# Modulated norms that take 1 + scale ahead of the inverse root, modulation weights in two loads, ones added on ScalarE, and a new hand-set priority table: an adaLN transformer block on one core

## The chip, the cores and the metric

The kernel runs on one core of a Trainium2 chip. Time is device time in microseconds (us) of that core. A profiled execution gives, beside the time, a trace with every instruction of TensorE (PE, with its weight loads as PEld), VectorE (DVE), ScalarE (ACT), GpSimd (POOL) and SyncE (SP, which only issues transfers here). All arithmetic that matters here is float32. One matmul of the program shows as two records in the trace: 87 fillers of the program are 174 records.

## The reference

Eight sequences of 1024 tokens by 128 features go through an attention stack of six layers and a quantized feed-forward part. Each part has a modulated norm in front and a gate behind; scale, shift and gate come from a conditioning vector of the sequence:

```python
mod = (_silu(L0_c) @ L0_wmod).reshape(L0_c.shape[0], 6, 1, -1)
sa, ca, ga, sb, cb, gb = (mod[:, 0], mod[:, 1], mod[:, 2], mod[:, 3], mod[:, 4], mod[:, 5])
...
h = _layernorm(x, axis=-1) * (1 + ca) + sa
x = x + ga * _L0_attn_ref(h, ...)
h = _layernorm(x, axis=-1) * (1 + cb) + sb
x = x + gb * _L0_ffn_ref(h, ...)
```

The attention part is six layers of norm, linear attention, norm and a two-layer MLP; the feed-forward part rounds blockwise to FP4 ahead of each of three matmuls. The modulated norm is thus computed twice for each sequence: once at its start, once ahead of the quantized part. The twelve norms inside the attention stack are plain ones whose weight and bias are folded in later.

## The kernel before

**Tiling.** One sequence is "a batch b" here. Its 1024 tokens are eight chunks of 128 tokens, and a half (h = 0, 1) is four chunks, so a half is a tile of 128 partitions by 512. Four batches are in flight at a time in four sets of buffers ("lanes"); the fifth to eighth reuse them.

**Order of the work.** The kernel does not issue its instructions as it describes them. Every step is put into a `Plan` with its engine, an estimated duration and what it reads and writes (`add`, L96). `Plan.order` (L143) then runs a list scheduler over these estimates. Of the steps that could start first it takes the one with the longest remaining chain plus a hand-set bonus. The bonuses are `LEAD[b][stage]`, changed at set times by `TURNS` (L291 to L360); a batch has eight stages: 0 is its modulated norm, 1 to 6 are the layers, 7 is the quantized part. The order that comes out is fixed: every engine runs its own list strictly in that order, and waits for what the others owe it.

**Fillers.** Where the scheduler expects PE to sit idle longer than `GAP` (0.6 us, half of that up to time `COLD`), it puts in matmuls of the identity by itself, whose result nobody reads (`warm`, L1348). They keep PE running while it has nothing to do. Fillers too are fixed parts of the list: PE runs them even if real work is ready earlier.

**The parts that the change touches.**
- The loads (L448 to L451): the conditioning vector, the first half of batch 0, all of the modulation weights `wmod` (384 KB), the second half of batch 0. All go out from the one SP queue, in this order, then every other weight.
- `prepare_mod` (L517): the modulation of all eight sequences as rows of 8 partitions. Two DVE instructions (L538) add 1 to the scales.
- `first_modulation` (L856): for the first four batches, scale and shift spread over the partitions by a matmul of `wmod`'s first 256 columns (L862), with two copies on ACT (L870, L871) that also add the 1.
- `layernorm` (L614): statistics on DVE (L630, L636), the inverse root as a logarithm and an exponential on ACT (L650, L655) and a correction of three small DVE instructions (L660, L665, L670), a fourth for the shift (L676); then the norm is applied, in chunks of 128 columns, by DVE (L682, mean and inverse root as two per-partition scalars) or by ACT (L689). The plain norms share a half between the two.
- `modulated_norm` (L887): a `layernorm`, then a multiply by 1 + scale on DVE over the whole half (L893) and an add of the shift on POOL (L901). At a batch's start the half is shared between DVE and ACT; ahead of the quantized part all four chunks are ACT's (the argument `HV` is 0).

```python
for h in range(H):
    layernorm(ln, dst, src, h, name, HV)
    add("DVE", vec(HW), ... tensor_tensor(half(dst, h), half(dst, h), over(mod[:, n + 1], HC), ALU.mult) ...)
    add("POOL", 1.2,    ... tensor_tensor(half(dst, h), half(dst, h), over(mod[:, n], HC), ALU.add) ...)
```

Of the kernel before, what the change touches and what calls it, by code (L numbers as in the profile page):

```python
# [11 lines left out]
ALU = mybir.AluOpType  # L12
# [71 lines left out]
class Plan:  # L84


    LAT = {"PE": 0.31, "ACT": 0.14, "DVE": 0.125, "POOL": 0.04, "SP": 2.0}
    SEE = {"PE": 0.015, "ACT": 0.0, "DVE": 0.0, "POOL": 0.1, "SP": 0.0}

    GAP, BRINK, COLD = 0.6, 0.15, 7.5  # L90

# [144 lines left out]
def mm(n):  # L236

    return 0.01 + n * 1.66e-3


def move(kb):

    return max(0.45, kb * 4.0e-3)

# [5 lines left out]
def kernel(  # L250
# [40 lines left out]
    LEAD = [  # L291
        [2420, 4178, 586, 336, -1174, -1157, -1341, -3664],
        [158, 557, 2162, 224, -3448, -84, 492, -1524],
        [1202, -253, -1456, -2344, -3625, 1683, -2362, -2313],
        [-238, 636, -1421, 177, -416, 253, -5410, -152],
# [7 lines left out]
        (15, [(2, 1, -124)]),  # L303
        (45, [(0, 2, 1600), (3, 0, -324)]),
        (60, [(1, 1, -935)]),
        (75, [(0, 3, 1449), (1, 1, 557), (3, 1, 592)]),
        (90, [(3, 1, 2100)]),
        (120, [(3, 2, 2464), (3, 3, 2879)]),
        (135, [(0, 3, 3161)]),
        (150, [(1, 1, 2636)]),  # L310
        (165, [(1, 2, 3857)]),
        (195, [(0, 4, 1947)]),
        (210, [(1, 3, 1937)]),
        (225, [(0, 4, 2875), (0, 6, 2412), (0, 7, 99)]),
        (240, [(2, 1, -1301), (3, 3, 1394)]),
        (255, [(0, 5, 2591), (1, 3, 3015), (1, 4, -653)]),
        (270, [(3, 4, 2428)]),
        (345, [(0, 6, 2433), (4, 0, -1503)]),
        (390, [(1, 4, -2461)]),
        (405, [(3, 6, -3105)]),  # L320
        (435, [(1, 4, -3419)]),
        (450, [(3, 6, -3090)]),
        (465, [(2, 2, 551), (2, 4, -3123), (3, 6, -3105)]),
        (510, [(4, 1, -3111)]),
        (525, [(3, 6, -3271)]),
        (540, [(3, 6, -3110)]),
        (600, [(3, 7, 2098)]),
        (615, [(2, 4, -3534)]),
        (630, [(2, 6, -2208), (5, 1, 1840)]),
        (660, [(5, 1, 1745)]),  # L330
        (690, [(5, 1, 2562)]),
        (720, [(4, 3, -2144)]),
        (750, [(2, 6, -2203)]),
        (780, [(2, 6, -2201), (2, 7, -2144), (4, 3, -2142), (5, 4, -2397)]),
        (810, [(2, 7, -2186)]),
        (825, [(3, 7, -2164), (4, 3, -1269)]),
        (840, [(3, 7, -2468)]),
        (870, [(3, 7, -340)]),
        (885, [(3, 7, -553), (4, 4, 939), (4, 5, 1955)]),
        (915, [(5, 4, -1086), (6, 2, -534)]),  # L340
        (945, [(4, 6, 1221)]),
        (975, [(4, 7, -240), (7, 1, -1371)]),
        (990, [(6, 3, 282)]),
        (1005, [(4, 7, -743), (5, 4, -650)]),
        (1035, [(4, 7, -1539), (5, 5, -1458)]),
        (1050, [(5, 5, -591), (6, 3, 867), (6, 4, 1080), (7, 2, 307)]),
        (1095, [(6, 4, -754)]),
        (1110, [(6, 4, -1551)]),
        (1125, [(4, 7, -4373), (6, 4, -758)]),
        (1140, [(6, 5, -1624)]),  # L350
        (1200, [(5, 7, -1877)]),
        (1215, [(6, 5, -185), (7, 4, -2011)]),
        (1230, [(6, 5, -1795)]),
        (1245, [(6, 6, -373), (7, 5, -366)]),
        (1260, [(6, 6, -371), (7, 5, -372)]),
        (1275, [(6, 6, -365), (7, 5, -367)]),
        (1305, [(6, 7, -440), (7, 6, -443)]),
        (1320, [(7, 6, 40)]),
        (1335, [(4, 7, -2064), (5, 7, -2271), (6, 7, -2282), (7, 6, 278), (7, 7, 207)]),
    ]  # L360
# [88 lines left out]
    load_x(0, 0)  # L449
    load(lambda: wmod_b.ap()[:, :NM], wmod, [wmod_b], 384)  # L450
    load_x(0, 1)  # L451
    for n, src in enumerate((ln1_w, ln1_b, ln2_w, ln2_b)):
        load(lambda n=n: rows[n * L : (n + 1) * L, :], src, [("rows", n)], 3)
# [63 lines left out]
    def prepare_mod():  # L517
        for o, e in MS:
            u = Ps(psum)
            add(  # L520
                "PE", mm(e - o),
                lambda u=u, o=o, e=e: nc.tensor.matmul(
                    u.ap()[:B, : e - o], cT, wmod_b.ap()[:, o:e],
                    start=True, stop=True,
                ),
                r=["cT", wmod_b], w=[u],
            )
            add(
                "ACT", act(e - o),
                lambda u=u, o=o, e=e: nc.scalar.copy(flat8[:, o:e], u.ap()[:B, : e - o]),  # L530
                r=[u], w=[("mod8", o)],
            )

        shaped = [("mod8", o) for o, _ in MS]
        for n in (1, 4):
            add(
                "DVE", 0.14,
                lambda n=n: nc.vector.tensor_scalar(  # L538
                    mod8[:, n, :], mod8[:, n, :], 1.0, None, ALU.add
                ),  # L540
                r=shaped, w=[("mod", n)], port=True,
            )
# [70 lines left out]

    def layernorm(ln, dst, src, h, n, HV=HC // 2):  # L614

# [5 lines left out]

        def s(c):
            return chunks(half(src, h))[:, c, :]

        def d(c):
            return chunks(half(dst, h))[:, c, :]

        for c in range(HC):
            add(
                "DVE", 0.197, lambda c=c: nc.vector.bn_stats(stats.ap()[:, c, :], s(c)),  # L630
                r=at(src, h)[c * H // HC :][:1], w=[stats[c]],
            )

        def moments():
            for c in range(HC):
                nc.vector.bn_aggr(mv.ap()[:, c, :], stats.ap()[:, c, :])  # L636

        add("DVE", HC * 0.067, moments, r=[stats], w=[mv])

# [3 lines left out]
        def var():  # L643
# [27 lines left out]
            r=[shift], w=[rstd], port=True,  # L671
        )

        add(
            "DVE", 0.07,
            lambda: nc.vector.scalar_tensor_tensor(z(), mean(), -1.0, y(), ALU.mult, ALU.mult),  # L676
            r=[mv, rstd], w=[shift], port=True,
        )

# [7 lines left out]
        def apply_s():  # L687
# [8 lines left out]
            "ACT", (HC - HV) * (act(D, 2) + 0.04), apply_s, r=[*at(src, h), shift, rstd],  # L696
            w=[high] if HV else [low, high],
        )
        if HV:
            add("DVE", HV * 0.256, apply_v, r=[*at(src, h), mv, rstd], w=[low], port=True)  # L700

# [13 lines left out]
    def fp4(src, parts, ncol, n, i, last="POOL"):  # L715
# [13 lines left out]
        def each(t):  # L729
# [49 lines left out]
        add(  # L779
            last, (vec if last == "DVE" else pool2)(ncol),  # L780
            lambda: eng.tensor_tensor(blocks(src()), blocks(vv()), each(s()), ALU.mult),
# [74 lines left out]
    def first_modulation(mod, b):  # L856


        t = Ps(psum)
        add(  # L860
            "PE", mm(2 * D),
            lambda: nc.tensor.matmul(  # L862
                t.ap()[:, : 2 * D], cT[:, b : b + 1].to_broadcast([P, P]),
                wmod_b.ap()[:, : 2 * D], start=True, stop=True,
            ),
            r=["cT", wmod_b], w=[t],
        )

        def spread():
            nc.scalar.copy(mod.ap()[:, 0, :], t.ap()[:, :D])  # L870
            nc.scalar.activation(mod.ap()[:, 1, :], t.ap()[:, D : 2 * D], AF.Identity, bias=1.0)  # L871

        add("ACT", 2 * act(D), spread, r=[t], w=[mod[0]], func="exp")
# [12 lines left out]

    def modulated_norm(ln, dst, src, mod, n, name, HV):  # L887

        for h in range(H):
            layernorm(ln, dst, src, h, name, HV)  # L890
            add(
                "DVE", vec(HW),
                lambda h=h: nc.vector.tensor_tensor(  # L893
                    chunks(half(dst, h)), chunks(half(dst, h)),
                    over(mod.ap()[:, n + 1, :], HC), ALU.mult,
                ),
                r=[mod[n // 3]], w=at(dst, h), port=True,
            )
            add(
                "POOL", 1.2,  # L900
                lambda h=h: nc.gpsimd.tensor_tensor(  # L901
                    chunks(half(dst, h)), chunks(half(dst, h)),
                    over(mod.ap()[:, n, :], HC), ALU.add,
                ),
                r=[mod[n // 3]], w=at(dst, h),
            )

# [18 lines left out]
    def layer(x, b, l, ln, mod):  # L926
# [197 lines left out]
        if l == L - 1:  # L1124
# [3 lines left out]
            add(  # L1128
                "POOL", pool2(NJ * D) + 0.1,
                lambda: nc.gpsimd.tensor_tensor(  # L1130
# [4 lines left out]
            for h in range(H):  # L1135
# [8 lines left out]
                add(  # L1144
                    "POOL", pool2(HW) + 0.2,
                    lambda h=h: nc.gpsimd.tensor_tensor(
# [44 lines left out]
    def ffn(x, mod, b, ln):  # L1191
        hq = big(ln, "A", f"h_{b}")
        modulated_norm(ln, hq, x, mod, 3, f"f{b}", 0)
        hT = big(ln, "B", f"hTf_{b}")
# [123 lines left out]
    for b in range(B):  # L1318
# [11 lines left out]
        x = big(ln, "X", f"x_{b}")  # L1330
        modulated_norm(ln, x, x0s[b], mod, 0, f"i{b}", HC // 2)
        for l in range(L):
# [77 lines left out]
```

## Time and profile before

| what | value |
|---|---|
| median of 3 runs | 1406.71 us (1405.73 to 2585.54) |
| the profiled execution, time | 1406.12 us |
| its span, first to last instruction | 1404.4 us |
| PE busy | 1391.3 us, 99% |
| DVE, ACT, POOL busy | 1142.5 us (81%), 983.0 us (70%), 247.7 us (18%) |
| granted TensorE clock | 0.999 |
| fillers | 174 records (87 matmuls) |
| PE idle over the span | 1404.4 - 1391.3 = 13.1 us |

The span is the time between the first and the last instruction that the profile holds; the time of the run is 1.7 us longer. Busy shares are averages over stages with different limits: at the start DVE is the fuller engine, from about 47 us on PE hardly pauses. A PE that is busy can be busy with fillers, which are not work.

### The profile page before, as it was taken

The page shows a single profiled execution, that of the slowest core. Times are in us where ns is not written, and L with a number is a line of the kernel's source. Part 1 is how long each engine was busy: PE and PEld are TensorE (multiplying, and loading weights), DVE is VectorE, ACT ScalarE, POOL GpSimd, SP SyncE. Part 2 cuts the span into 40 slices and gives each one's busy share as a digit, 9 for nine tenths or more (in the row PEclk, how much of TensorE's full clock was granted, in tenths as well). Part 3 has the DMA queues.
Part 4 walks back from the last instruction along what each step waited for, and adds up shares of the span by engine and source line. Part 5 has one row for each costly group of instructions (what it writes and reads, how often), then busy time and mean ns, then how long its engine had stood idle before and what let it go on. Part 6 is the DMA issues. An engine that isn't in the chain of part 4 may idle for free.

```text
span 1404.4 us, 26348 instructions
## 1 busy us (share of the span) xinstructions
PE 1391.3 (99%) x9181; PEld 1116.3 (79%) x9181; DVE 1142.5 (81%) x4506; ACT 983.0 (70%) x2292; POOL 247.7 (18%) x216
## 2 busy tenths in 40 slices
PE   8999999999999999999999999999999999999998
PEld 6788779688768888688788778788787787887887
DVE  8998668487798687899667899988876748879897
ACT  6777666766686686767666668876776757777774
POOL 2211001001122020312101122211210101212232
PEclk9999999999999999999999999999999999999999
DMA  7100000000000000100000000000000000000001
GB/s 218 47 1 1 2 1 1 0 1 1 17 12 16 1 2 1 42 16 13 2 0 1 16 13 16 1 16 1 1 1 1 1 1 1 2 1 1 9 17 38
DMA packets 16293, 18.79 MB, mean 13 GB/s; under 512 B 1584, under 2 KB 10392, under 8 KB 16160
## 3 DMA queue, kind: packets, MB, share of 16 engines
q1 hardware_dynamic: 16160, 17.10, 3.9%
q8 instruction: 73, 1.20, 0.4%
q14 instruction: 60, 0.49, 0.1%
HBM read 12.88 MB, written 4.22 MB: 12 GB/s over the span
## 4 chain that ended last, share of the span: by engine, by line
PE 88%; DVE 7%; ACT 2%; SPq 1%; DMA 1%; issue 1%; POOL 0%; POOLq 0%; ACTq 0%; DVEq 0%
PE ps L1178 22%; PE ps L1161 22%; PE ps L708 11%; PE ps L1048 6%; PE ps L938 5%; PE ps L1115 5%; PE ps L985 5%; PE ps L1222 5%; PE ps L1302 3%; PE ps L1278 1%; SPq L417 1%; DVE x L1100 1%; PE ps L1082 1%; PE ps L1057 1%; DMA x<-in_L_attn_x_dram 1%; DVE stats_m L630 1%
## 5 line engine op out<-in xcount | busy, mean ns | idle before, releaser
L1161 PE MATMUL ps<-xT_m,w_sb 128*128 128x512 f32 x768 | 352.0, 595 | 0.3 <-ACT xT_m L918 0.3
L1161 PEld LDWEIGHTS ps<-xT_m,w_sb 128*128 128x128 f32 x768 | 137.6, 191 | 128.8 <-issue 95.6
L1026 POOL TENSOR_TENSOR q<-q,qsum 128x512 f32<-128x512 f32 x96 | 102.4, 1075 | 709.2 <-DVE qsum L1021 377.2
L1100 DVE TENSOR_TENSOR x<-ps,x 128x512 f32<-128x512 f32 x192 | 129.7, 680 | 105.2 <-PE ps L1178 81.1
L985 PEld LDWEIGHTS ps<-wq_sb,xT_a 128*128 128x128 f32 x768 | 96.4, 192 | 26.3 <-issue 18.9
L689 ACT ACTIVATE xh_a<-x,shift_a,rstd_a 128x128 f32<-128x128 f32 x192 | 83.6, 487 | 34.6 <-DVE shift_a L676 33.4
L1115 PEld LDWEIGHTS ps<-m,qT 128*128 128x128 f32 x768 | 92.3, 192 | 11.1 <-issue 4.3
L985 PE MATMUL ps<-wq_sb,xT_a 128*128 128x128 f32 x768 | 98.8, 275 | 0.0
L1178 PEld LDWEIGHTS ps<-w_sb,hT_D 128*128 128x128 f32 x640 | 86.6, 192 | 14.3 <-issue 11.2
L938 PE MATMUL ps<-xT_a,wk_sb 128*128 128x512 f32 x192 | 96.1, 597 | 1.6 <-ACT xT_a L918 1.6
L1178 PE MATMUL ps<-w_sb,hT_C 128*128 128x128 f32 x640 | 97.6, 275 | 0.0
L1178 PE MATMUL ps<-w_sb,hT_E 128*128 128x128 f32 x640 | 97.6, 275 | 0.0
L1178 PE MATMUL ps<-w_sb,hT_B 128*128 128x128 f32 x640 | 97.6, 275 | 0.0
L1178 PE MATMUL ps<-w_sb,hT_D 128*128 128x128 f32 x640 | 97.5, 275 | 0.0
L1115 PE MATMUL ps<-m,qT 128*128 128x128 f32 x768 | 95.9, 275 | 0.1
L689 ACT ACTIVATE xh_m<-x,shift_m,rstd_m 128x128 f32<-128x128 f32 x192 | 81.8, 487 | 17.8 <-DVE shift_m L676 17.6
L1048 PEld LDWEIGHTS ps<-k,xh_a 128*128 128x128 f32 x768 | 90.4, 192 | 4.2 <-issue 2.2
L1048 PE MATMUL ps<-k,xh_a 128*128 128x128 f32 x768 | 93.4, 275 | 0.0
L650 ACT ACTIVATE rstd_a<-mv_a,eps 128x4 f32<-128x4 f32 x96 | 28.1, 296 | 88.2 <-DVE mv_a L636 84.1
L630 DVE BATCH_NORM_STATS2 stats_a<-x 128x6 f32<-128x128 f32 x384 | 84.9, 279 | 3.5 <-POOL x L901 1.7
L918 ACT ACTIVATE xT_m<-ps,cols 128x512 f32<-128x512 f32 x96 | 72.1, 776 | 20.1 <-PE ps L708 20.0
L1178 PEld LDWEIGHTS ps<-w_sb,hT_B 128*128 128x128 f32 x640 | 84.5, 192 | 1.0 <-issue 1.0
(181 smaller groups left out, 3229.8 us busy)
## 6 DMA issues: line engine op xcount, KB each, us to landing
x<-in_L_attn_x_dram SPq DMA_DIRECT2D x16, 256.0 KB, 3.4
out_dram<-x SPq DMA_DIRECT2D x14, 256.0 KB, 2.0
w_sb<-in_L_attn_w_dram SPq DMA_DIRECT2D x12, 256.0 KB, 4.4
mod<-mod_d SPq DMA_DIRECT2D x8, 256.0 KB
mod<-mod_d SPq DMA_DIRECT2D x4, 128.0 KB
out_dram<-x SPq DMA_DIRECT2D x4, 128.0 KB
wmod_b<-in_L_wmod_dram SPq DMA_DIRECT2D x1, 384.0 KB, 4.1
wk_sb<-in_L_attn_wk_dram SPq DMA_DIRECT2D x6, 64.0 KB, 4.1
```

The source lines that it names most:

```text
L630: "DVE", 0.197, lambda c=c: nc.vector.bn_stats(stats.ap()[:, c, :], s(c)),
L689: nc.scalar.activation(d(c), s(c), AF.Identity, bias=shift.ap()[:, c : c + 1], scale=rstd.ap()[:, c : c + 1],)
L708: nc.tensor.transpose(t.ap()[:, c * P : (c + 1) * P], chunks(half(src, h))[:, c, :], ident)
L918: lambda t=t, h=h: nc.scalar.activation(half(xT, h), t.ap(), AF.Identity, bias=col(params + 1, l), scale=col(params, l),),
L938: lambda tk=tk, h=h: nc.tensor.matmul(tk.ap(), wk_sb[:, l, :], half(xT, h), start=True, stop=True),
L985: nc.tensor.matmul(tq.ap()[:, c * D : (c + 1) * D], half(xT, h)[:, c * P : (c + 1) * P], wq_sb[:, l, :], start=True, stop=True,)
L1026: lambda h=h, hs=hs: nc.gpsimd.tensor_tensor(heads(half(q, h)), heads(half(q, h)), each(qsum.ap()[:, hs]), ALU.mult),
L1048: nc.tensor.matmul(tc_.ap()[:, :D], chunks(xh.ap())[:, c, :], chunks(k.ap())[:, c, :], start=(c == 0), stop=(c == C - 1),)
L1100: lambda: nc.vector.tensor_tensor(half(x, h), t.ap(), half(x, h), ALU.add),
L1115: nc.tensor.matmul(to.ap()[:, c * D : (c + 1) * D], half(qT, h)[:, c * P : (c + 1) * P], m.ap(), start=True, stop=True,)
L1161: lambda th=th, h=h, j=j: nc.tensor.matmul(th.ap(), w1_sb[:, l, j * P : (j + 1) * P], half(xmT, h), start=True, stop=True,),
L1178: nc.tensor.matmul(ty.ap()[:, c * D : (c + 1) * D], hidden(j)[:, c * P : (c + 1) * P], w2g.ap()[:, j, :] if l == L - 1 else w2_sb[:, l, j, :],
```

## The change

Four things change.

1. `modulated_norm` no longer calls `layernorm`. Statistics and inverse root are in a function of their own, `moments`. The norm is then two products in another order: first (x - mean) * (1 + scale), which needs no inverse root, by one DVE instruction for each chunk; then times the inverse root. For batch 0's first norm and batch 7's second one (`quick`) the latter is a second DVE instruction for each chunk that also adds the shift, with POOL left out. Everywhere else ACT multiplies by the inverse root, chunk by chunk, and POOL adds the shift as before.
2. `wmod` is loaded as two transfers: 128 KB between the two halves of batch 0, 256 KB after the second. `first_modulation` waits for the first alone.
3. The two additions of 1 in `prepare_mod` go from DVE to ACT.
4. The scheduler's estimates (`LAT` of SP, `COLD`, `mm`, `move`, a few POOL durations) and its bonuses (one entry of `LEAD`, all of `TURNS`) are others, so the order of every engine's list is another one from near the start to the end.

```diff
-    LAT = {"PE": 0.31, "ACT": 0.14, "DVE": 0.125, "POOL": 0.04, "SP": 2.0}
+    LAT = {"PE": 0.31, "ACT": 0.14, "DVE": 0.125, "POOL": 0.04, "SP": 2.6}
-    GAP, BRINK, COLD = 0.6, 0.15, 7.5
+    GAP, BRINK, COLD = 0.6, 0.15, 11.5
...
 def mm(n):
-    return 0.01 + n * 1.66e-3
+    return 0.0115 + n * 1.654e-3
 def move(kb):
-    return max(0.45, kb * 4.0e-3)
+    return max(0.45, kb * 3.6e-3)
...
-        [1202, -253, -1456, -2344, -3625, 1683, -2362, -2313],
+        [3230, -253, -1456, -2344, -3625, 1683, -2362, -2313],
...
     load_x(0, 0)
-    load(lambda: wmod_b.ap()[:, :NM], wmod, [wmod_b], 384)
+    load(lambda: wmod_b.ap()[:, : 2 * D], wmod[:, : 2 * D], [wmod_b[0]], 128)
     load_x(0, 1)
+    load(lambda: wmod_b.ap()[:, 2 * D : NM], wmod[:, 2 * D :], wmod_b.parts[1:], 256)
...
-                "DVE", 0.14,
-                lambda n=n: nc.vector.tensor_scalar(
-                    mod8[:, n, :], mod8[:, n, :], 1.0, None, ALU.add
-                ),
-                r=shaped, w=[("mod", n)], port=True,
+                "ACT", act(D) + 0.1,
+                lambda n=n: nc.scalar.activation(
+                    mod8[:, n, :], mod8[:, n, :], AF.Identity, bias=1.0
+                ),
+                r=shaped, w=[("mod", n)],
...
-    def modulated_norm(ln, dst, src, mod, n, name, HV):
+    def modulated_norm(ln, dst, src, mod, n, name, quick):
         for h in range(H):
-            layernorm(ln, dst, src, h, name, HV)
-            add("DVE", vec(HW), ... ALU.mult ...)
-            add("POOL", 1.2, ... ALU.add ...)
+            mv, rstd = moments(ln, src, h, name)[:2]
+            def first(cs, chunk=chunk, mv=mv):
+                for c in cs:
+                    nc.vector.scalar_tensor_tensor(
+                        chunk(dst, c), chunk(src, c), mv.ap()[:, c, 0:1],
+                        mod.ap()[:, n + 1, :], ALU.subtract, ALU.mult,
+                    )
+            def second(cs, chunk=chunk, rstd=rstd):
+                for c in cs:
+                    nc.vector.scalar_tensor_tensor(
+                        chunk(dst, c), chunk(dst, c), rstd.ap()[:, c : c + 1],
+                        mod.ap()[:, n, :], ALU.mult, ALU.add,
+                    )
+            def scaled(cs, chunk=chunk, rstd=rstd):
+                for c in cs:
+                    nc.scalar.mul(chunk(dst, c), chunk(dst, c), rstd.ap()[:, c : c + 1])
...
+                add("DVE", Q * vec(D), lambda f=first, cs=cs: f(cs), ...)
+                if quick:
+                    add("DVE", Q * vec(D), lambda f=second, cs=cs: f(cs), ...)
+                else:
+                    add("ACT", Q * act(D, 1), lambda f=scaled, cs=cs: f(cs), ...)
+            if not quick:
+                add("POOL", 1.3, ... ALU.add ...)
...
-        modulated_norm(ln, hq, x, mod, 3, f"f{b}", 0)
+        modulated_norm(ln, hq, x, mod, 3, f"f{b}", b == B - 1)
...
-        modulated_norm(ln, x, x0s[b], mod, 0, f"i{b}", HC // 2)
+        modulated_norm(ln, x, x0s[b], mod, 0, f"i{b}", b == 0)
```

The lists of the two kernels, engine by engine, hold the same matmuls but for the fillers. These are the places of the fillers, counted in program matmuls:

| stretch of PE's list | before | after |
|---|---|---|
| up to the first transposes of batch 0 | 1 + 4 + 41 | 2 + 2 + 25 |
| from there to the first MLP matmul of layer 0 | 3 + 2 + 2 + 3 | 2 + 2 |
| from there to the last batch's end phase | 2 | 3 + 3 |
| the end phase | 7 + 3 + 5 + 2 + 4 + 4 + 2 + 2 | 3 + 3 + 3 + 4 + 2 + 4 + 5 + 2 + 2 |
| all | 87 | 67 |

The other lists differ in the kinds and numbers that the diff names: DVE gets 144 of the new three-operand instructions and loses 32 of L682, 32 of L893, 32 of L676 and the 2 of L538; ACT loses 96 of L689 and gets 112 multiplications by the inverse root and the 2 additions of 1, and switches its function table 29 times instead of 31; POOL loses 4 of L901; SP gets one transfer more.

## The prediction

> **What bounds the kernel now.** I read the page's busy line, then the windows by stage, then PE's waits, then the timeline of the first 47 us, where the change puts most of its work.
>
> ```profile
> PE 1391.3 (99%) x9181; PEld 1116.3 (79%) x9181; DVE 1142.5 (81%) x4506; ACT 983.0 (70%) x2292; POOL 247.7 (18%) x216
> ```
>
> PE is busy 99%. Its idle time is 1404.4 - 1391.3 = 13.1 us, and 87 of its matmuls are fillers. From the timeline, 82 filler records take 11.67 to 20.83, so one program matmul takes 9.16 / 41 = 0.223 us; 82 warm ones are 18.3 us, the five cold ones about 2.6. Fillers and idle are thus 34 us, and no reordering can give more than 34 us of 1404. Most of that is fixed: the lead-in.
>
> ```profile
> 0.00:21.00 21.00, 18.12 (x106) 14.05 (x107) 15.12 (x98) 11.36 (x35) 5.14 (x14) 1.00 0.70 220
> 21.00:47.00 26.00, 23.85 (x163) 19.20 (x161) 25.94 (x117) 19.11 (x55) 7.17 (x6) 1.00 0.61 178
> 47.00:100.00 53.00, 53.00 (x386) 45.20 (x386) 51.97 (x240) 42.89 (x110) 13.77 (x12) 1.00 0.01 2
> 1375.00:1404.40 29.40, 25.03 (x176) 21.20 (x175) 23.97 (x54) 11.92 (x30) 7.03 (x6) 1.00 0.08 28
> ```
>
> Columns: stretch, length, busy PE, PEld, DVE, ACT, POOL. From 21 to 47 us DVE works 25.94 of 26: there DVE is the bound, not PE, whose 23.85 still hold ten fillers. From 47 us on PE is full, and DVE still nearly so.
>
> ```profile
> 11.67 9.32 PE L1350 MATMUL warm<-ident 128*128 128x128 f32 x82
> 20.83 1.04 PE L708 MATMUL ps<-ident,xh_a 128*128 128x128 f32 x8
> 46.93 7.13 PE L1161 MATMUL ps<-xT_m,w_sb 128*128 128x512 f32 x16
> ```
>
> Batch 0's first transposes start at 20.83, and the first MLP matmul at 46.93; from there PE has a backlog. Between 47 and 1375 us it waits hardly at all (columns: total, times, longest):
>
> ```profile
> PE ps L938 <- ACT xT_a L918: 1.3, 2, 1.1
> PE ps L708 <- DVE xh_m L682: 1.3, 1, 1.3
> PE ps L1161 <- ACT xT_m L918: 0.3, 1, 0.3
> PE ps L708 <- DVE shift_a L660: 0.2, 1, 0.2
> PE ps L1082 <- DVE ctxT L1074: 0.2, 1, 0.2
> ```
>
> That is 3.3 us in 1328. So a change in the middle can only lose by much; what can be won lies before 47 us and in the last 40.
>
> **The lead-in, part by part.** The split load: the first half of x lands at 4.70, wmod's 384 KB at 5.88 and the second half at 6.45, so 256 KB are worth about 0.7 us and 128 KB 0.4. After it, the part of wmod that the first modulation needs should land at 5.1, the second half at 5.8. Yet PE's list puts batch 2's modulation ahead of batch 0's, at a cold 0.98 us each (before: two in 2.04 us), and its two copies come first on ACT as well, with a logarithm between. Batch 0's scale is then ready at 5.1 + 2.1 + ACT's 0.6 = about 7.8, while DVE is through with both halves' statistics at 6.9. Its idle time behind 4.70 is 1.0 us, against (6.45 - 5.77) + (7.68 - 7.23) = 1.1 before: nothing won, nothing lost. The extra transfer costs the SP queue one issue of 0.43 us, which every later load stands behind. What waits for those is DVE's statistics of batches 2 and 3, which have other rows around them; I cost it at nothing, 0.4 if that cover is gone. The two ones-additions on ACT (as L871, 0.28 each) fall where ACT waits for the second norm's statistics (2.57 us idle before L650 at 14.97): nothing, 0.6 without it.
>
> **DVE up to 46.93.** Since DVE has no gap there, I sum its list up to the last chunk of the second norm (row 129 in both lists), in start-to-start times of the timeline. Gone: 12 of L682 at 0.26 (a pair is 0.52), 4 of L893 at 0.60, 6 of L676 at 0.07, one subtraction 0.60, one bias row 0.20, one ones-addition 0.13: together 6.9 us. Added: 4 statistics at 0.195, 8 aggregations at 0.07, one maximum over 512 with its small partner 0.66: 2.0 us. And 24 of the new three-operand instructions with one per-partition scalar. No such row on SBUF alone exists; near it are (columns behind the bar: busy us, mean ns, idle before)
>
> ```profile
> L1089 DVE SCALAR_TENSOR_TENSOR m<-ps,ksum,mb_bc 128x128 f32<-128x128 f32 x48 | 16.3, 341 | 7.4 <-PE ps L1082 7.3
> L682 DVE TENSOR_SCALAR xh_a<-x,mv_a,rstd_a 128x128 f32<-128x128 f32 x192 | 59.5, 353 | 0.5 <-PE ps L1161 0.5
> L600 DVE SCALAR_TENSOR_TENSOR mb_bc<-mb_bc,ps 128x128 f32<-128x128 f32 x6 | 1.5, 272 | 0.0
> ```
>
> L1089 has the same form, with one operand in PSUM; the next instruction starts 0.26 us after it (34.77 to 35.03). L600, without a per-partition scalar, takes 0.20. So the bounds are 0.20 and 0.26, and I take 0.26 of the nearer row. (The scheduler reckons with 0.1985.) That is 24 x 0.26 = 6.2, and DVE's sum is 2.0 + 6.2 - 6.9 = +1.4 us (0.0 at 0.20).
>
> The Trainium skill's "VectorE: DVE Perf Modes", section "The perf-mode tier table", speaks against this exchange: in float32 an instruction with one tensor runs at twice the rate of one with two (1227 against 2293 ns at 2048 columns). At 128 columns that is an estimated 0.07 us, so by the rule a new instruction would cost 0.26 + 0.07 = 0.33, and the sum be +3.0. The rows don't show the difference (L682 has two per-partition scalars, L1089 one and a second tensor; both 0.26), so I stay with 0.26, and keep 0.33 for the range.
>
> Against it stands a hold-up:
>
> ```profile
> 10.31 1.55 DVE L682 TENSOR_SCALAR x<-x,mv_i,rstd_i 128x128 f32<-128x128 f32 x2
> 10.41 1.37 POOL L901 TENSOR_TENSOR x<-x,mod 128x512 f32<-128x512 f32 x1 [7.28 <-DVE shift_i L676]
> ```
>
> This pair takes 1.55 where others take 0.60, for as long as POOL adds: 0.95 us lost. Batch 0 has no POOL add afterwards. The other two hold-ups of this stretch (DVE at 40.00 and 43.15) belong to POOL's w2g, which stays. DVE then reaches the first MLP matmul +1.4 - 0.95 = 0.4 us later. But PE has by then done 8 transposes more (layer 0 of batch 2), 2 x 0.44 = 0.9 us. Head: **0.5 us won** (1.9 at 0.20; 1.1 lost at 0.33). PE has 23 fillers fewer in this stretch, 5.1 us, but they were not what it waited for: nearly all of it turns into idle time. The transposes themselves start earlier, I reckon near 19 us, for what follows DVE just as before.
>
> **The middle.** DVE in all: 144 x 0.26 - 32 x 0.26 - 32 x 0.60 - 32 x 0.07 - 0.3 = +7.4 us, 82% instead of 81; covered by its 260 us of idle. Were that cover gone where DVE is full (95.87 of 100 us between 800 and 900), PE would wait for some of it, at most 7. ACT loses 96 of L689 (0.39 apart) and gets 112 with one scalar less (like L607, 0.40 long against 0.48, so some 0.31): -2.7 us, and two table loads of 1.28 less; off the path. POOL loses 4 x 1.27. SP's moved loads of later batches are far ahead of use. Fillers from there to the end: 34 against 31, **0.7 us lost**. PE's waits of 3.3 us: between 0 and double. The new estimates agree better with this trace (mm(128) 0.2225 to 0.2232, measured 0.2234; half speed till 11.5 instead of 7.5, in the trace till about 11.6), so the list should be better timed: I take half, **1.6 us won**.
>
> **The end.** Batch 7's second norm loses ACT's 1.65, L893's 0.69 and POOL's 1.27 for four DVE instructions of 1.04: 2.6 us shorter for each half. What stood there was a run of 7 fillers (1366.58), now 3; that is in the count above. What is late next is the same chain of rounding, transposes and last matmuls with 22 fillers before and 25 after. Nothing more.
>
> **Sum.** 1406.1 (this profiled execution's time: 1404.4 and 1.7 around it) - 0.5 + 0.7 - 1.6 = 1404.7. The median of the runs is 0.6 above that execution: **1405 us**.
>
> **Rivals.**
> - *The fillers are the time.* If DVE has slack in the head after all, 20 fillers go with their time (20 x 0.223 = 4.5) and the middle's waits too: 1398 to 1400. For it: the order is made by timing PE's gaps, and expects fewer. Against: 25.94 of 26.
> - *DVE's head gets longer* (slower). The place is 7 to 100 us, where DVE is full; price: at 0.33 each the head loses 1.1, the 16 to 20 such instructions of batches 1 and 3 that follow by 100 us another 1.3, and each microsecond in which DVE now waits (for batch 0's scale, or for ACT, which has the exponential of the second half queued behind two chunks of the first) comes on top, 2 to 4: 1409 to 1412. It decides from the point where DVE's sum is more than 0.9 us over the one before, as then the 8 extra transposes no longer pay.
> - *The new order starves PE in the middle.* 28 us are needed for 2%, 21 times the longest wait there. By the skill's "TensorE: Matmul & The Clock Gate" (section "What's actually happening") an idle PE falls to half clock after about 3.4 us; no run here shows it past the start. A stall of that length with as much work at half speed behind it costs 5.1 us, so five or six would do it: 1435 and more.
> - *The split brings nothing*, as batch 2 goes first: that is already in the sum.
>
> **How the numbers follow.** Main case 0.50 (1401 to 1408), fillers 0.22 (1398 to 1401), DVE's head 0.24 (1408 to 1413), starved PE 0.04. Of each side case I leave about a third to lie beyond its outer end; with the starved case that is 0.19 outside 1398 to 1413. A measurement of this kernel tells 2% from no change, 28 us: faster by that is out of reach (0.01, as the 34 us can't all go), slower 0.04, within 0.95.
>
> **What would show it.** Right: first transposes at 18.5 to 20; first MLP matmul at 46 to 48; DVE above 25 of 26 us from 21 to 47; new instructions 0.26 apart; PE idle up by 4 to 5 us before 47, fillers down by 20; waits from 47 to 1375 under 4 us. Wrong: the MLP at 44 or 49, or a PE wait over 2 us in the middle.

## The result, and the profile after

| | before | after |
|---|---|---|
| median | 1405.11 us (9 runs: 1404.07 to 1406.71, and one of 2585.54) | 1409.34 us (9 runs, 1408.65 to 1410.62) |
| ratio, 95% interval | | 1.003, 1.0021 to 1.0039 |
| span of the profiled execution, granted clock | 1404.4 us, 0.999 | 1407.3 us, 0.996 |

The change costs 0.3%: 4.2 us by the medians, 2.9 by the two profiled executions. 1405 was forecast, a small gain. The range held the time, but the sign was wrong, so the small terms of the sum are what has to be explained.

The page's busy line of the changed kernel, then its windows by stage (stretch, length, busy PE, PEld, DVE, ACT, POOL; the third number from the end is the granted clock):

```profile
PE 1390.0 (99%) x9141; PEld 1112.5 (79%) x9141; DVE 1139.7 (81%) x4552; ACT 976.0 (69%) x2308; POOL 243.0 (17%) x212
```

```profile
0.00:21.00 21.00, 15.54 (x78) 10.91 (x78) 15.83 (x100) 9.52 (x29) 2.50 (x12) 0.98 0.75 218
21.00:47.00 26.00, 22.25 (x144) 17.97 (x144) 24.98 (x127) 20.10 (x65) 5.99 (x5) 0.89 0.60 181
47.00:100.00 53.00, 52.34 (x365) 44.06 (x366) 48.28 (x209) 42.92 (x108) 14.61 (x13) 0.97 0.01 2
1375.00:1407.30 32.30, 27.74 (x188) 23.06 (x186) 26.45 (x63) 12.30 (x30) 7.14 (x7) 1.00 0.09 33
```

PE does less in all, and yet the kernel is slower. Two things are new here: DVE, which was busy for 25.94 of the 26 us from 21 to 47, now stands still for 1.0 us; and the clock is below 1.00 in the first three stretches, where it was 1.00 before. The timeline of PE for the same work that was shown of before (in brackets the idle time ahead, and what ended it):

```profile
15.97 0.85 PE L722 MATMUL ps<-ident,xh_a 128*128 128x128 f32 x4
18.23 1.03 PE L722 MATMUL ps<-ident,xh_a 128*128 128x128 f32 x4 [1.40 <-DVE xh_a L697]
22.76 0.56 PE L583 MATMUL ps<-cols,wv_sb 128*128 128x1 f32 x2 [3.49 <-issue]
23.18 1.20 PE L1395 MATMUL warm<-ident 128*128 128x128 f32 x4
24.66 3.09 PE L983 MATMUL ps<-xT_a,wk_sb 128*128 128x512 f32 x4 [0.29 <-ACT xT_a L963]
...
47.29 0.99 PE L722 MATMUL ps<-ident,xh_m 128*128 128x128 f32 x4 [1.33 <-DVE q L1046]
48.93 7.98 PE L1206 MATMUL ps<-xT_m,w_sb 128*128 128x512 f32 x16
```

The first transposes come at 16.0 and 18.2 us instead of 20.8: the new norm does bring batch 0 forward. Then PE waits 3.5 us and loses the lead. The first projection (L983) starts at 24.66, 2.4 us later than before (22.30), and takes 3.09 us for what took 1.98. The first MLP product comes at 48.93 instead of 46.93, and its sixteen records take 7.98 instead of 7.13 us.

What PE waits for at 22.76 stands in the timelines of DVE and ACT:

```profile
21.95 0.64 DVE L636 BATCH_NORM_AGGREGATE mv_i<-stats_i 128x2 f32<-128x6 f32 x8
22.49 0.17 DVE L518 COPY cols<-ps 128x24 f32<-128x24 f32 x1
```

```profile
21.03 2.45 ACT L927 ACTIVATE x<-x,rstd_i 128x128 f32<-128x128 f32 x8 [1.96 <-DVE rstd_i L670]
...
23.86 1.42 ACT L963 ACTIVATE xT_a<-ps,cols 128x512 f32<-128x512 f32 x2
```

`cols` holds the norms' weights and biases as columns. It is one DVE copy of 0.17 us, whose input PE makes ahead of the long run of fillers. DVE's list has it behind batch 2's norm and batch 1's statistics. ACT needs it to turn batch 0's transposes into `xT_a`, and has that turn behind batch 2's eight multiplications. Before, the copy stood at 20.28, where nothing was waiting yet.

Where do the 2.9 us of the two executions go? Each span is cut here at its first MLP product, first before, then after:

```profile
46.93:1404.40 1357.47, 1349.39 (x8916) 1083.13 (x8915) 1101.51 (x4294) 952.57 (x2204) 235.43 (x196) 1.00 0.02 7
```

```profile
48.93:1407.30 1358.37, 1350.53 (x8914) 1082.16 (x8912) 1096.92 (x4321) 945.31 (x2214) 233.22 (x194) 1.00 0.02 7
```

2.0 us are lost ahead of that product. Behind it the difference is 0.9, and the sixteen slow records alone are 7.98 - 7.13 = 0.85. So the remaining 1350 us, with their other lists and fillers, look equal. They are not, since the profiled execution of before has a stretch at half clock of its own there (two rows of PE, then a window):

```profile
794.31 1.68 PE L708 MATMUL ps<-ident,xh_m 128*128 128x128 f32 x8 [1.25 <-DVE xh_m L682]
796.32 8.83 PE L1161 MATMUL ps<-xT_m,w_sb 128*128 128x512 f32 x16 [0.34 <-ACT xT_m L918]
```

```profile
796.54:799.95 3.41, 3.41 (x5) 1.35 (x5) 3.27 (x19) 0.99 (x2) 0.00 (x0) 0.50 0.00 0
```

Sixteen such records take 7.03 us at full clock, so this stretch cost up to 1.80 us. Not every execution of before has one: of the 86 that were timed beside the experiments, the 59 with a mean clock of 1.000 took 1404.88 us in the median, and the 27 below it 1406.45. Without it, the stretch of 1357.47 us would be about 1355.7 (an estimate, 1357.47 - 1.80), and the changed kernel loses more behind its first MLP product than the two traces show at first sight.

### The profile page after: what moved, and what is told of

Same layout as the page of the kernel before. It is cut to its first block, busy times and chain, and to the rows that moved or that the text cites. A ratio compares the mean times of both kernels' runs of the same rounds, so it can differ in the third digit from the quotient of the medians.

```text
span 1407.3 us, 26292 instructions
## 1 busy us (share of the span) xinstructions
PE 1390.0 (99%) x9141; PEld 1112.5 (79%) x9141; DVE 1139.7 (81%) x4552; ACT 976.0 (69%) x2308; POOL 243.0 (17%) x212
## 4 chain that ended last, share of the span: by engine, by line
PE 83%; DVE 13%; ACT 3%; issue 1%; DMA 0%; POOL 0%; SPq 0%; DVEq 0%; ACTq 0%; POOLq 0%
PE ps L1206 22%; PE ps L1223 21%; PE ps L722 11%; PE ps L1160 5%; PE ps L1093 5%; PE ps L1030 5%; PE ps L983 5%; PE ps L1267 4%; PE ps L1347 2%; DVE x L1145 1%; PE ps L1323 1%; DVE stats_m L628 1%; PE ps L1102 1%; PE ps L1127 1%; DVE h L913 1%; DVE stats_a L628 1%
## 5 line engine op out<-in xcount | busy, mean ns | idle before, releaser
L983 PE MATMUL ps<-xT_a,wk_sb 128*128 128x512 f32 x192 | 95.5, 601 | 0.7 <-ACT xT_a L963 0.7
L1006 ACT ACTIVATE kT<-ps,nmax 128x512 f32<-128x512 f32 x96 | 65.2, 684 | 41.6 <-DVE nmax L997 41.5
L963 ACT ACTIVATE xT_a<-ps,cols 128x512 f32<-128x512 f32 x96 | 71.9, 773 | 22.8 <-PE ps L722 22.3
```

Of the source, the lines that this page charges most:

```text
L963: lambda t=t, h=h: nc.scalar.activation(half(xT, h), t.ap(), AF.Identity, bias=col(params + 1, l), scale=col(params, l),),
L983: lambda tk=tk, h=h: nc.tensor.matmul(tk.ap(), wk_sb[:, l, :], half(xT, h), start=True, stop=True),
```

## Experiments

In ten of the twelve kernels the lists that the planner makes for the changed kernel are kept, and only named steps are moved within one engine's list (`shift_to`: ahead of a step, `put_behind`: after one), or fillers are put in ahead of a step. Line numbers shift by a few.

### The copy of cols and ACT's turn (e1, e2, e3)

```diff
 ordered = plan.order(LEAD, TURNS, warm)
+shift_to("DVE", named["cols"], named["firsti2"][0])
...
+shift_to("ACT", named["xTa0_0"], named["scaledi2"][0])
```

The first line is e1, the second e2, both are e3.

> Only the copy of cols on DVE is moved, from behind batch 2's norm to ahead of it (about 22.5 to 18.3 us). Theory A (DVE's order alone holds PE): PE's product of L583 comes at 18.9 instead of 22.8, PE's wait of 3.5 us goes, the first projection starts near 20 and the time falls by 2 us or more, to 1407 or less. Theory B (ACT's order holds it as well): the turn to xT_a stays at 23.9 behind batch 2's eight multiplications, the wait only changes its place (to the projection, still at 24.7 us), and the time stays within 0.5 us of 1409.3.

Measured: 1409.54 us, ratio 1.0030 (1.0017 to 1.0042). The wait moves, as theory B has it:

```profile
24.93 3.78 PE L990 MATMUL ps<-xT_a,wk_sb 128*128 128x512 f32 x4 [4.42 <-ACT xT_a L969]
```

> Only ACT's two turns to xT_a are moved, ahead of batch 2's eight multiplications; the copy of cols stays late, at 22.5 us. If ACT's order alone is the fault: the turn starts at 22.8 instead of 23.9, the projection at 23.5 instead of 24.7, and the time falls by about 1 us, to 1408.3. If the copy of cols is what all waits for: ACT now stands still until 22.7, batch 2's multiplications end near 26.6 instead of 23.5, DVE's statistics of batch 2 (23.7 us, with the maximum of L990 queued behind them) wait some 3 us, and the time rises by 1 to 3 us, to 1410.3 to 1412.3.

Measured: 1410.12 us, 1.0037 (1.0024 to 1.0049), just under the range of the second case. The row of DVE that pays for it:

```profile
26.69 0.87 DVE L631 BATCH_NORM_STATS2 stats_a<-x 128x6 f32<-128x128 f32 x4 [2.93 <-POOL x L951]
```

> Both moves. ACT then turns xT_a at about 19.1 to 20.5 us, before batch 2's multiplications can start (21.0), so nothing is displaced, and PE's first projection starts near 20.3 instead of 24.7 us. If PE's chain sets the start of the MLP: first MLP product near 44.5 to 45 us instead of 48.9, time 1405 to 1405.5. If DVE's list sets it (the maximum of L990 keeps its place, at best 26.0 instead of 26.8): MLP no earlier than 47.5 to 48, time 1408 to 1408.5. If PE still falls to half clock while it waits for DVE, 1409.

Measured: 1407.78 us, 1.0019 (1.0012 to 1.0027): 1.6 us of the 4.2 come back. The projection starts 4.0 us earlier, at 20.66, but the MLP only 0.7 us earlier, at 48.26: nearest to the second case. PE now waits for DVE's maximum, which keeps its place in DVE's list:

```profile
20.66 2.62 PE L990 MATMUL ps<-xT_a,wk_sb 128*128 128x512 f32 x4
...
28.62 1.79 PE L725 MATMUL ps<-ident,kT 128*128 128x128 f32 x8 [3.21 <-ACT kT L1013]
```

So both orders are at fault together, neither alone; and behind them DVE's list is the next limit.

### Where the clock falls, and what it costs (e4, e5, e6, e9)

The granted clock of the changed kernel, in windows (PE's busy time is the third number):

```profile
16.00:19.00 3.00, 1.54 (x10) 0.87 (x8) 3.00 (x23) 2.02 (x9) 0.00 (x0) 1.00 0.95 225
19.00:22.00 3.00, 0.26 (x1) 0.07 (x1) 3.00 (x19) 1.04 (x5) 0.00 (x0) 0.68 0.54 172
24.00:26.00 2.00, 1.71 (x4) 0.90 (x4) 1.75 (x14) 1.97 (x7) 0.90 (x1) 0.50 0.93 289
28.00:45.00 17.00, 16.47 (x128) 14.49 (x128) 17.00 (x83) 13.26 (x43) 3.20 (x3) 1.00 0.54 163
49.00:51.00 2.00, 2.00 (x4) 0.89 (x3) 2.00 (x9) 1.08 (x5) 0.00 (x0) 0.54 0.00 0
51.00:53.00 2.00, 2.00 (x6) 0.88 (x5) 1.71 (x8) 2.00 (x6) 0.00 (x0) 1.00 0.00 0
```

PE runs at half clock twice, from about 20 to 27 us and from 47 to 51. The first suspect was the wait of 3.5 us:

```diff
+fillers(named["bv0"][0], 14, (5,))
```

> Fourteen fillers of 0.22 us stand ahead of PE's product of L583, in its wait of 3.5 us; nothing else is changed. If the drop of the clock to half (0.50 in 22 to 26 us) comes from that wait and costs time: clock 1.00 in 22 to 28 us, the four projection records take 2.0 instead of 3.1 us, DVE's wait of 0.93 us before its maximum goes, the time falls by 0.9 us, to 1408.4. If the slow stretch is hidden under DVE's list: clock 1.00 but time 1409.3 within 0.3. If the clock stays at 0.5 all the same, idleness is not its cause.

Measured: 1416.24 us, 1.0079 (1.0066 to 1.0092), none of the three cases.

```profile
19.43 11.51 PE L1402 MATMUL warm<-ident 128*128 128x128 f32 x28
```

Two readings. The fillers begin at 19.43, and the clock falls at 19.65 all the same: its cause lies ahead of the wait. And fourteen fillers that all write one PSUM bank take 0.82 us each at half clock, where those at 23.18 in the changed kernel take 0.60; they were meant to fill 3.5 us and took 11.5. The run says nothing on what the slow stretch costs.

So the fillers went into the gaps ahead of it, in several banks by turns, in e3's lists (e5) and in the changed kernel's own (e9, the first two lines alone; `kt` are the transposes of kT):

```diff
+fillers(named["turna0_0"][0], 2, (3, 4))
+fillers(named["turna0_0"][1], 6, (5, 6, 3, 4))
+fillers(kt, 10, (7, 0))
```

> The kernel of e3, with fillers in three of PE's gaps of the head, in four banks or two by turns: two ahead of the first transposes of xh_a (16 us), six ahead of the second (17 to 18.4), ten in the wait for kT (25.4 to 28.6). If the clock fell in e3 (0.50 in 19 to 22 us and in 29 to 31) because PE had done nothing but transposes and idling for some three microseconds: clock 1.00 from 12 to 50 us. If a stretch at half clock in the head costs time by itself, the start of the MLP falls from 48.3 to 47.5 or less and the time by 0.7 or more against e3, to 1407.0; if DVE's list sets the start, the clock is 1.00 and the time stays within 0.4 of e3's 1407.8. If the clock falls all the same, transposes and idling are not the cause.

Measured: 1406.75 us, 1.0011 (1.0004 to 1.0017): 1.0 us below e3, with the clock at 1.00 throughout, as in the first case. DVE then has no gap at all, and the MLP starts at 47.50:

```profile
16.00:47.00 31.00, 27.00 (x188) 22.26 (x189) 31.00 (x166) 23.39 (x75) 6.96 (x6) 1.00 0.64 184
47.50:1405.10 1357.60, 1349.74 (x8914) 1081.91 (x8912) 1097.75 (x4324) 945.47 (x2214) 233.37 (x194) 1.00 0.02 7
```

> The changed kernel with eight fillers alone: two ahead of the first transposes of xh_a and six ahead of the second (16 to 18.4 us), in four banks by turns; the copy of cols and ACT's turn stay late. If the first drop of the clock (0.50 from about 20 to 27 us) comes from PE's transposes and idling after 16 us, and not from its later wait for cols: the clock stays 1.00 to 22 us at least. If it then holds through the four projections (3.1 us at half clock, 2.0 at full): DVE's wait of 0.93 us for them goes, the MLP starts 0.9 us earlier and the time is 1408.4. If the wait of 3.5 us for cols lets the clock fall by itself, it falls a few us later and the time stays within 0.4 of 1409.3.

Measured: 1409.30 us, 1.0027 (1.0016 to 1.0038): the last case.

```profile
16.00:19.00 3.00, 2.94 (x22) 2.19 (x19) 3.00 (x23) 2.03 (x9) 0.00 (x0) 1.00 0.89 255
19.00:22.00 3.00, 0.24 (x1) 0.05 (x1) 3.00 (x19) 1.05 (x5) 0.00 (x0) 1.00 0.58 173
22.00:26.00 4.00, 3.01 (x8) 2.19 (x9) 3.72 (x30) 3.97 (x15) 2.49 (x2) 0.54 0.88 262
```

With fillers from 16 to 19 us the clock holds until 22.3; then the wait for `cols` brings it down by itself. Thus the first fall comes from the gaps of 16 to 19 us, in which PE has little but eight transposes, and the wait would have caused it too. It takes the order and the fillers together (e5) to be rid of it.

For the second fall, five fillers were put ahead of the second transposes of `xh_m`:

```diff
+fillers(named["turnm0_0"][1], 5, (6, 1))
```

> The changed kernel with nothing but five fillers in two banks by turns ahead of the second transposes of xh_m (PE's wait of 1.33 us at 46 us). If the second drop of the clock (0.54 in 47.3 to 50.7 us) comes from that gap and costs what the trace suggests (0.7 ahead of the first MLP product and 0.85 in the sixteen after it): clock 1.00 there, sixteen records in 7.1 instead of 8.0 us, time 1407.7. If it is hidden, or comes from something else, 1409.3 within 0.4.

Measured: 1412.02 us, 1.0051 (1.0038 to 1.0063). It tells nothing on its question, since the fillers' bank was not free:

```profile
49.33 2.19 PE L1402 MATMUL warm<-ident 128*128 128x128 f32 x10 [2.03 <-DVE mb_bc L606]
```

The answer came from e3, e5 and e9, whose clock stays full there with about the same wait (1.32 to 1.81 us): the sixteen MLP records take 7.03 us in all three, against 7.98. That is 0.95 us, and most of it reaches the end: from the first MLP product to the end are 1358.37 us in the changed kernel, and 1357.60 to 1357.64 in e3, e5 and e9.

### The planner's list as a whole (e7, e8)

e7 has all edits of the change with the `LEAD` (in which two entries differ, 1202 and -3664), `TURNS` and costs of before; e8 is the changed kernel in which the copy of `cols` is ranked first.

```diff
 prepare_c()
+plan.lead = 1e6
 prepare_cols()
+plan.lead = -LATE
```

> All of the change's edits (the modulated norm, the load of the modulation's weights in two parts, the ones on ACT) with the kernel before's leads, turns and planner's costs. If the lists made from the new leads and costs lose the 4 us: 1404 to 1406, no half clock after the start, PE without a wait over 2 us in the head. If the edits themselves lose it (DVE's longer sum in the head): 1408 to 1410 here too. The plan for the middle is then another one, so 1 us more or less tells nothing.

> The changed kernel, where only the lead of the copy of cols in the planner is raised, so that it is ranked first; all lists are made anew (copy at row 10 of DVE instead of 56, the first product with cols among the first fillers). If the late copy is what the planner gets wrong: PE without a wait over 2 us in 16 to 25 us, the MLP's first product at 46.5 to 47.5 us at full clock and 1405 to 1407. If DVE's list has no room however it is ordered: MLP at 48 or later, 1407.5 to 1409.

Measured: 1462.13 us (1.0407, 1.0392 to 1.0421) and 1487.14 us (1.0587, 1.0572 to 1.0601). Both expectations fail: 57 and 82 us over before. Yet both heads are the best of all; e7, then e8:

```profile
43.19 7.03 PE L1204 MATMUL ps<-xT_m,w_sb 128*128 128x512 f32 x16
```

```profile
44.08 7.03 PE L1206 MATMUL ps<-xT_m,w_sb 128*128 128x512 f32 x16
```

What they lose comes later: 490 and 612 filler records instead of 134, so 178 and 239 program fillers more (40 and 53 us at 0.223 each), and PE idle for 19 and 24 us behind the first MLP product, where it was 8 before. The bonuses seem fitted to one exact course of the list: one changed priority at 12 us gave other lists to the end, and worse ones. Hence these two kernels can't tell what the edits by themselves are worth. But the start of the MLP is not bound to DVE's whole list up to there: another order has it at 43.

### Is DVE's sum a limit, or only its order? (e10, e11, e12)

e10 takes e5 and moves 2.2 us of batch 3's statistics on DVE behind the work for the first MLP product (`mom_v`, with ACT's roots `mom_s`). e11 also moves one subtraction ahead of the norm of `xh_m`, which frees the PSUM bank that PE waits for at 46 us. e12 is e5 with that last move alone.

```diff
+put_behind("DVE", mom_v, named["q2_0"][3])
+put_behind("ACT", mom_s, named["scaledi1"][1])
+put_behind("DVE", named["rooti3"][0::3], named["moma1_0"][4])
...
+put_behind("DVE", named["q2_0"][1:2], named["q2_0"][0])
```

> The kernel of e5, and batch 3's statistics with their aggregates (eight and two instructions, 2.2 us of DVE, half of it at 23 us) are moved on DVE behind the last work that the first MLP product waits for; ACT's roots of batch 3 go behind its first leaky evictions. Nothing else moves. If the start of the first MLP product is what fixes the time (in the runs so far the span less that start is 1357.5 to 1358.5 us, where the clock was full): the start falls from 47.5 to about 45.3, the time by about 2, to 1404.7. If DVE's sum has to be paid anyway, ahead of the MLP or soon after it: PE waits in 50 to 70 us instead, the span less the start grows by 2, and the time stays at 1406.7.

> The kernel of e10, and DVE's first subtraction for lane 2's q is moved ahead of the norm of xh_m, so that the PSUM bank is free that PE's second transposes of xh_m wait for (the wait of 1.33 us). If that wait is a matter of the bank: it falls to 0.7 or less, the MLP starts about 0.6 us before that of e10, the time is 1404.1, 1.0 below the kernel before. If the norm itself comes late by as much as it is pushed back: same as e10.

Measured: 1409.49 us (1.0029, 1.0018 to 1.0041) and 1409.37 us (1.0026, 1.0015 to 1.0036), worse than e5 by 2.6 to 2.7. In e10 the start of the MLP stays at 47.49. Part of the time taken out of DVE's list comes back at once as a wait, since batch 2's chain through ACT and POOL is late next; and PE waits later for what was pushed back:

```profile
24.29 0.87 DVE L631 BATCH_NORM_STATS2 stats_a<-x 128x6 f32<-128x128 f32 x4 [1.11 <-POOL x L953]
```

```profile
PE ps L1216 <- DVE mb_bc L606: 0.9, 1, 0.9
PE ps L1112 <- ACT gxk L1109: 0.8, 1, 0.8
PE ps L727 <- POOL q L1081: 0.6, 1, 0.6
PE ps L992 <- ACT xT_a L971: 0.4, 1, 0.4
```

These are PE's waits from 47 to 85 us; PE is idle for 38 - 35.39 = 2.6 us there, in e5 for 0.4. What was taken out in front of the MLP was paid again by 85 us.

> The kernel of e5, and DVE's first subtraction for lane 2's q is moved ahead of the norm of xh_m, without the move of batch 3's statistics. PE's wait of 1.33 us for that PSUM bank goes or falls to 0.2, the MLP starts 0.6 us before that of e5 (46.9 instead of 47.5). If in lists that are otherwise kept the start of the MLP fixes the time: 1406.1, and the span less the start stays 1357.6. If DVE's sum up to some 80 us is the limit instead: the start comes earlier, PE waits as much more later, and the time stays at 1406.7.

Measured: 1406.69 us, 1.0010 (1.0003 to 1.0016), the same as e5 within 0.1. The wait for the bank falls to 0.29 and the MLP starts 0.5 us earlier:

```profile
44.44 1.75 PE L727 MATMUL ps<-ident,xh_m 128*128 128x128 f32 x8 [0.29 <-DVE xh_m L702]
...
47.01 7.13 PE L1216 MATMUL ps<-xT_m,w_sb 128*128 128x512 f32 x16
```

In the profiled executions 0.2 of these 0.5 us arrive at the end, in the medians less than 0.1. So an earlier MLP alone is not time won: from its start to the end are 1357.60 to 1357.64 us in e3, e5 and e9, and 1357.89 in e12. No version here beats the kernel before.

## Why the prediction was wrong, and where it was right

**The first step that failed: the lead-in and what follows it.** 0.5 us were to be won ahead of the first MLP product, and 2.0 were lost. The prediction says that the transposes start "near 19 us, for what follows DVE just as before", and the head is then a sum over DVE's list. A sum over an engine's list is its time only if that engine never waits. The transposes came earlier than forecast, but the first consumer of their result needs `cols`, and two lists, DVE's and ACT's, had put batch 2 in front of it. DVE then waited 0.9 us for PE's projection: 24.98 of 26, where "above 25" was to be seen. I summed DVE's rows, and did not follow batch 0's chain through the other two lists. In e5, where order and clock are mended and DVE has no gap, the MLP starts at 47.50; the sum had 46.93 + 0.4 = 47.3. That is near, but the sum is no bound: e12 has 47.01 and e7 43.19.

**The fillers.** That "nearly all of it turns into idle time" was right in amount: from 16 to 47 us PE is idle for 31 - 24.05 = 6.95 us, before for 2.15, so 4.8 more. What was wrong is that this was costed at nothing. The idle time cost the clock: 3.09 instead of 1.98 us for the projection DVE waits for, and 0.85 to 0.95 us in the first MLP records. The rule on the clock was cited in the prediction, but only for the rival of long stalls in the middle, and with the words that no run shows it past the start. The trace of before shows it at 796.54 us, behind the wait of 1.3 us for `xh_m` that the prediction lists.

**The second step that failed: the middle.** "1.6 us won" by better-timed lists did not come; about as much was lost. From the first MLP product to the end are 1357.60 us in e5, all at full clock, and before 1357.47 with the slow stretch or about 1355.7 without it (the estimate above): 1.9 us more. The median times say 1.3: at full clock e5 takes 1406.73 us and before 1404.88, so e5 is 1.85 longer, and 0.57 of that is its later MLP. e12, whose MLP starts only 0.08 us later than before, is still 1.8 us longer. PE's idle time behind the first MLP product is 8.1 us before and 7.9 in e5, so what grew is PE's busy time: 1349.74 us against about 1349.39 - 1.80 = 1347.6, where eight transposes less (each is one record, unlike the other matmuls) and three fillers more were to make -0.2. Which steps of the new lists cost it is open. Better estimates in a planner were no evidence of a better list.

**What held, and what else did not.** The new DVE instruction: two take 0.62 us and four 1.14 in the timeline, so 0.26 apart, as taken; the 0.33 worked out from the Trainium skill ("VectorE: DVE Perf Modes", section "The perf-mode tier table") is not borne out for this form. Waits from 47 to 1375 us are 4.0 us, of which 1.3 belong to the head (47.29). The end phase: from the start of the last eight matmuls with `wguT` to the end 23.85 us before and 23.48 after. DVE's busy time in all did not hold: it was to rise by 7.4 us and fell from 1142.5 to 1139.7, for a reason that is open.

**The rivals.** "DVE's head gets longer" gave 1409 to 1412, and the time lies there, in part by luck: its price of 0.33 for an instruction did not come, and of the waits of DVE that it put on top, with ACT's order as one place, 1.0 us came against its 2 to 4. The half clock and the longer middle it did not name. "The fillers are the time" fell: the fillers went, and the time with them did not.

**By the medians** the change costs 4.2 us. The two orders give back 1.6 (e3) and the clock 1.0 more (e5); 1.6 are left that no experiment gave back. In e5 about 0.6 of that lies ahead of the first MLP product, and the rest is the longer middle. The load in two parts, the ones on ACT and the new norm were not undone one by one: e7, the one kernel that has them under the planner's settings of before, takes another course to the end. So their own price is not shown.

## What to carry to other kernels

Where in-order lists are made by a planner, a step that brings one chain forward is worth only what the small shared steps on that chain allow: follow the chain through every engine's list and look at what stands ahead of each consumer, before adding up the bound engine's rows. Fillers that are removed are not free because PE had nothing to do; look at what follows the gap, and whether it is on the path at half clock. A list whose priorities are fitted to one course should be changed by moving single steps; in e7 and e8 a new course cost far more than the edit under test. And before two profiled executions are subtracted, compare their clocks stretch by stretch: here a slow stretch of before hid a loss of about the same size.

## What the runs showed of the hardware

**The clock changes on a fixed grid.** Windows of 0.25 us around the four changes in the changed kernel (the clock is either 0.50 or 1.00, so the mean of a window gives the moment):

```profile
20.00:20.25 0.25, 0.00 (x0) 0.00 (x0) 0.25 (x3) 0.00 (x0) 0.00 (x0) 0.72 0.17 53
26.75:27.00 0.25, 0.25 (x1) 0.12 (x1) 0.22 (x1) 0.00 (x0) 0.00 (x0) 0.63 0.23 68
47.25:47.50 0.25, 0.21 (x2) 0.24 (x3) 0.25 (x1) 0.24 (x1) 0.00 (x0) 0.83 0.07 18
50.75:51.00 0.25, 0.25 (x2) 0.18 (x1) 0.25 (x3) 0.06 (x1) 0.00 (x0) 0.84 0.00 0
```

That is 20.11, 26.94, 47.42 and 50.83 us: distances of 6.83, 20.48 and 3.41, or 2, 6 and 1 times 3.41. The slow stretches of the other traces are multiples too: 3.4 in before, 6.8 in e9, 10.2 in e1, 13.7 in e4. This agrees with the Trainium skill ("TensorE: Matmul & The Clock Gate", section "What's actually happening"), which gives a free-running window of 3413 ns. So a gap of less than half a window can cost a whole one, if it falls badly: the wait of 1.33 us at 46 us did in the changed kernel, and about the same wait in e3, e5 and e9 did not. Before's wait of 1.25 us at 793 us did too, in the profiled execution; that other executions escape it because the grid lies elsewhere in them is likely, but not shown.

**How busy PE must be in a window, and with what.** Four windows of the grid: ahead of the fall at 47.42 in the changed kernel, ahead of the fall at 796.54 in before, and two in e9 and e12 that the clock survived. The last row is e12's window again, for the matmuls with `ident` alone, which there are all transposes:

```profile
44.00:47.42 3.42, 1.94 (x13) 1.26 (x13) 3.42 (x8) 3.18 (x8) 1.28 (x1) 1.00 0.56 177
793.13:796.54 3.41, 1.84 (x9) 1.17 (x10) 3.41 (x11) 2.58 (x6) 0.77 (x1) 1.00 0.00 0
46.20:49.60 3.40, 1.59 (x12) 1.31 (x10) 3.40 (x12) 2.56 (x6) 1.67 (x2) 1.00 0.25 81
42.94:46.35 3.41, 2.91 (x17) 1.68 (x17) 3.38 (x10) 2.69 (x8) 1.26 (x2) 1.00 0.63 200
42.94:46.35 3.41, 2.89 (x16) 1.00 0.63 200
```

A window with PE busy for 1.94 of 3.42 us lost the clock, and one with 1.59 kept it, so busy time alone does not decide between these two. The first held transposes alone and the second other matmuls too, but transposes can keep the clock up: e12's window (its clock is recorded from 8.81 us on, ten windows ahead of 42.94) held almost nothing else, for 2.91 us. The Trainium skill says on the same page that transposes don't count as PE-busy in the same way ("Part 4: PE-mode transpose"); e12's window speaks against it, as far as one window can.

**Fillers in one bank.** At half clock a program filler takes 1.20 / 2 = 0.60 us in the planner's own fillers (23.18 in the changed kernel), and 0.82 where all write one bank (e4); and the clock did not come back in the 11.5 us that they ran.
